# Layer 1's loop: num in the one-pass type with weights in two halves, carried rows through small transfers, and an own bank for the last columns

## The chip, the cores and the metric

The kernel runs on one core of a Trainium2 chip. The core has a matrix engine (PE, whose weight loads are listed apart as PEld), a vector engine (DVE), an activation engine (ACT), a general engine (POOL) and a queue engine that issues transfers (SP); ACT and POOL issue transfers too. All transfers run on the same 16 DMA engines. Matrix products land in PSUM, which has eight banks of 512 four-byte columns; DVE and ACT copy them to SBUF. The metric is the device time of one execution in microseconds. Three runs of the kernel before gave 651.62, 651.85 and 652.48, median 651.85.

## The reference

Two graph layers on 2708 nodes with 128 features and a dense 0/1 adjacency matrix; each ends in a layer norm. The change touches only the second one (layer 1):

```python
XW = X @ W
s_col = XW @ a[0, :f];  s_row = XW @ a[0, f:]
Z1  = leaky_relu(s_row[:, None] + s_col[None, :], 0.01)
den = exp(Z1)
num = A @ den
att = where(num != 0, den / where(num != 0, num, 1), 0)
H   = A @ (att @ XW)
out = layernorm(X + H)
```

`num` is a product of the adjacency matrix with a 2708 x 2708 matrix that depends on only two numbers per entry, s_row of one node and s_col of another.

## The kernel before

Exp(leaky_relu(a + b)) is either exp(a) exp(b) or exp(0.01 a) exp(0.01 b), and which of the two holds is decided by comparing b with -a. The kernel uses that. It sorts nodes by s_row (as "k") and by s_col (as "j") into NG = 24 groups of at most G = 126 nodes with common thresholds. Num can then be written as a running sum over the groups: for group g only the group's own 126 rows of the transposed adjacency matrix are needed, and everything outside the group is carried in two more rows, row 0 and row 1, which are the sums so far for the two branches. A group's product is therefore one 128 x 128 weight tile times a 128 x 2708 tile: 126 gathered rows plus two carried rows. Its first two output rows are the carried rows for the next group.

The stages ahead of the loop (layer 0, the sums over all nodes in `tot`, the sort, the tables) fill the first 345 us, and the last product H = A @ M with its layer norm takes the time from about 573 us on. The loop lies between them, at lines 1530 to 1589 (`for step in range(NG + LAG)`, LAG = 2).

Each step g does this. `multiply` (line 1460) forms num for six strips of 512 columns (the last has 148) with PE in the four-byte type, and DVE copies each from PSUM to the tile q. PSUM has three banks for that (`ps_num`) and five for the sums of the first five strips (`ps_m`). `carry` (1472) copies q's first two rows into rows 0 and 1 of the tile `ring` that holds the next group's gathered rows; this is one DVE instruction for three strips, twice a step. `log` (1476), on ACT, takes the logarithm of the step's q in two parts. `divide` (1480), on DVE, works on the step before: it subtracts the logarithm from the log of den. `power` (1488), on ACT, takes the exponential, in two parts and a third for the last 148 columns, which goes to a tile `tails`. `weigh` (1497) multiplies the quotient of two steps ago with that group's gathered rows of XW (`xws`) and adds it in PSUM to the sums m_acc, strip by strip. The last 148 columns have no bank of their own during the loop: `weigh_tails` multiplies all 24 of them at the end of it, in the bank m_tail. `weights` (1371) makes the weight tile of the group after next with one ACT instruction. Logarithm and exponential are in different tables of ACT, so there are two table loads a step.

POOL issues the loop's gathers: `gather` (1280), 126 rows of 10,832 bytes into one of four ring tiles, and `gather_xw` (1291), 128 rows of 512 bytes. For eleven steps it also issues a transfer that writes a two-byte copy of the first columns to HBM, and then one for `last_short`. Ring tile 0 is the room of the input x. SP issues the spread of the weights' row values over the partitions (`spread_out_weights`, 1413, for groups 4 to 7 and 8 to 23), and, as ring tiles, weights and XW rows come free, the first loads of the last product (line 1709).

The order of work on each engine is the order in the code: the helpers `mm`, `dve`, `act`, `gps` and `pinned` (lines 194 to 222) tie every instruction to the one before it on its engine, so that all of them appear under line 198 in the profile. Transfers on SP that are not pinned are placed by the scheduler by their estimated readiness. Elsewhere (`halves`, 224) a value is split into two halves of the one-pass type (F32R): the rounded value and the remainder. A product with both halves takes two one-pass products; the last product already does that with m_hi and m_lo.

## Time and profile before

| | |
|---|---|
| median of three runs | 651.85 us |
| profiled execution | 652.04 us, span 649.3 us, mean granted PE clock 0.984 |
| PE busy in the span | 608.8 us (94%) |
| DVE, ACT, POOL busy | 491.4, 471.3, 289.2 us |
| one step of the loop (from 424 us on) | 8.855 us |
| first product of num; last sums of m_acc | 345.6 us; 571.9 us |
| DMA | 171.64 MB, mean 264 GB/s |

The page sorts instructions into groups of one line, engine, operation and shape, with a count, the busy time and the mean of one; then comes the idle time of the engine before them and what ended it. A matmul of the four-byte type is two records. The records of matmuls overlap, since they are pipelined: what one costs is read from the distance between starts, not from its length. A window's row gives for each engine the busy time and the number of instructions in that stretch, then the granted clock of PE, the busy share of the DMA engines and their rate. The chain lists, in order of time, the work that set the end. A DMA row gives the time from issue to landing.

### The profile page before, as it was taken

What the parts mean: (1) busy time and instruction counts of PE and PEld (TensorE: products, weight loads), DVE (VectorE), ACT (ScalarE), POOL (GpSimd) and SP (SyncE); (2) the same over time, 40 slices, a digit from 0 to 9 for tenths busy, and PEclk for the clock granted to TensorE, in tenths of its full rate; (3) what the DMA queues carried; (4) which work ended last, traced back from release to release, by engine and by line L of the source; (5) the groups of instructions that cost most, each with busy time, mean ns of one, the idle gap of its engine ahead of it and who ended that gap; (6) DMA issues with size and microseconds to landing.
All of it is one profiled execution on the core that took longest, in us unless ns stands there. A gap on an engine that the chain in (4) does not pass through costs nothing.

```text
span 649.3 us, 8555 instructions
## 1 busy us (share of the span) xinstructions
PE 608.8 (94%) x2859; PEld 351.9 (54%) x2859; DVE 491.4 (76%) x978; ACT 471.3 (73%) x649; POOL 289.2 (45%) x270
## 2 busy tenths in 40 slices
PE   7999999999999899998878899999999999989993
PEld 4445345465655676765664344444444444658872
DVE  5765865764699756756885999899999999599575
ACT  4767786767889521410585999999999999778652
POOL 6967778777798742000123322333232230021573
PEclk9999999999999899999988999999999999999997
DMA  8968989988971999989956999756689453259981
GB/s 270 392 221 330 317 301 363 360 329 310 335 262 70 276 390 389 387 267 375 394 205 185 238 223 246 214 168 175 193 217 267 170 170 129 87 202 383 390 320 53
DMA packets 66407, 171.64 MB, mean 264 GB/s; under 512 B 10059, under 2 KB 19285, under 8 KB 63333
## 3 DMA queue, kind: packets, MB, share of 16 engines
q1 hardware_dynamic: 42500, 107.01, 46.4%
q0 software_dynamic: 22464, 62.25, 34.5%
q10 hardware_dynamic: 1392, 1.77, 0.8%
q8 instruction: 24, 0.39, 0.2%
q14 instruction: 27, 0.21, 0.1%
HBM read 171.89 MB, written 5.72 MB: 274 GB/s over the span
## 4 chain that ended last, share of the span: by engine, by line
PE 65%; ACT 13%; DVE 10%; POOL 6%; issue 4%; DMA 1%; another core or an unknown queue 0%; DVEq 0%; POOLq 0%; ACTq 0%
PE num L198 11%; PE m_acc L198 11%; PE att_acc L207 9%; PE h_acc L1690 7%; PE sim L207 7%; PE dif_acc L207 6%; ACT q L198 5%; POOL total L222 4%; ACT L198 2%; DVE q L198 2%; PE tot L198 2%; PE dif_acc L198 1%; PE sim L198 1%; POOL ss L198 1%; ACT xn L198 1%
## 5 line engine op out<-in xcount | busy, mean ns | idle before, releaser
L198 PE MATMUL m_acc<-q,xws 128*128 128x512 f32 x240 | 121.6, 592 | 0.0
L198 PE MATMUL num<-ring,wt 128*128 128x512 f32 x216 | 98.2, 546 | 3.6 <-DVE q L198 2.2
L222 POOL TENSOR_TENSOR total<-total,p_t 128x512 f32<-128x512 f32 (+1 forms) x67 | 91.8, 1370 | 21.0 <-ACT p_t L217 18.4
L207 PE MATMUL att_acc<-p_t,x_sb 128*128 128x512 f32 x184 | 91.1, 602 | 1.1 <-ACT p_t L217 1.1
L212 DVE SCALAR_TENSOR_TENSOR p_t<-sim,gentle,pieces 128x512 f32<-128x512 f32 x89 | 65.0, 746 | 34.8 <-PE sim L207 25.7
L198 DVE SCALAR_TENSOR_TENSOR q<-sr_b,nc_s,q 128x1536 f32<-128x1536 f32 (+1 forms) x48 | 77.8, 1623 | 17.3 <-ACT q L198 17.3
L217 ACT ACTIVATE p_t<-p_t,shift 128x512 f32<-128x512 f32 (+1 forms) x89 | 64.7, 745 | 33.8 <-DVE p_t L212 31.5
L198 DVE COPY q<-num 128x512 f32<-128x512 f32 (+1 forms) x142 | 83.5, 611 | 4.5 <-PE num L198 4.5
L198 PEld LDWEIGHTS m_acc<-q,xws 128*128 128x128 f32 x240 | 45.3, 190 | 55.0 <-issue 54.8
L198 ACT ACTIVATE q<-q,head,rest 128x1536 f32<-128x1536 f32 (+1 forms) x48 | 70.2, 1508 | 1.6 <-DVE ring L198 1.3
L198 ACT ACT_TABLE_LOAD x52 | 66.7, 1283 | 3.9 <-issue 3.1
L198 PEld LDWEIGHTS num<-ring,wt 128*128 128x128 f32 x216 | 39.0, 190 | 49.1 <-issue 34.2
L198 ACT ACTIVATE q<-q,c_s 128x1536 f32<-128x1536 f32 (+1 forms) x48 | 62.9, 1355 | 0.3
L198 POOL DMA_INDIRECT ring<-in_adj_t,k_no x18 | 20.8, 1154 | 89.1 <-PE num L198 85.6
L207 PEld LDWEIGHTS att_acc<-p_t,x_sb 128*128 128x128 f32 x184 | 31.7, 189 | 35.3 <-ACT p_t L217 18.8
L207 PE MATMUL sim<-xn_t 128*128 128x512 f32 x98 | 47.6, 592 | 0.0
L222 POOL TENSOR_TENSOR x<-x,p_t 128x660 f32<-128x660 f32 (+1 forms) x22 | 35.1, 1596 | 11.3 <-ACT p_t L217 10.6
L198 ACT ACTIVATE row<-row 128x1354 f32<-128x1354 f32 x30 | 39.5, 1318 | 0.3 <-DMA row<-in_adj 0.3
L207 PE MATMUL dif_acc<-strip,x_hi 128*128 128x512 f32 x88 | 37.8, 429 | 0.0
L207 PE MATMUL dif_acc<-strip,x_lo 128*128 128x512 f32 x88 | 36.2, 411 | 0.0
L1690 PE MATMUL h_acc<-rounded,m_hi 128*128 128x512 f32 x88 | 32.4, 407 | 3.7 <-DVE rounded L212 3.7
L198 PE MATMUL num<-x_sb,wt 128*128 128x512 f32 (+1 forms) x72 | 34.4, 570 | 0.7 <-ACT gb L198 0.7
(362 smaller groups left out, 1170.6 us busy)
## 6 DMA issues: line engine op xcount, KB each, us to landing
pieces<-in_adj_t SPq DMA_DIRECT2D x24, 1024.0 KB, 6.8
strip<-in_adj_t POOLq DMA_DIRECT2D x20, 1024.0 KB, 18.3
row<-in_adj SPq DMA_DIRECT2D x30, 677.0 KB, 5.5
nat<-in_adj_t SPq DMA_DIRECT2D x19, 768.0 KB, 7.7
x<-in_adj SPq DMA_DIRECT2D x14, 677.0 KB, 6.2
ring<-in_adj_t SPq DMA_DIRECT2D x9, 1024.0 KB, 5.1
pieces<-in_adj_t SPq DMA_DIRECT2D x7, 512.0 KB, 6.4
x_sb<-in_adj_t SPq DMA_DIRECT2D x4, 768.0 KB, 6.2
```

What stands on the lines that cost most here:

```text
L198: latest[engine] = op(*args, **kwargs)
L207: op(*args, **kwargs)
L212: return getattr(nc.vector, op)(*args, **kwargs)
L217: return getattr(nc.scalar, op)(*args, **kwargs)
L222: return getattr(nc.gpsimd, op)(*args, **kwargs)
L1690: nc.tensor.matmul(acc[:, : rows.shape[-1]], m[:, kb, :], rows, start=(kb, part) == (0, 0), stop=(kb, part) == (NB - 1, 1),)
```

## The change

- A group has GK = 124 gathered "k" rows instead of 126, because four carried rows take the first places instead of two: rows 0 and 1 in a rounded half and the remainder of each. The j groups keep 126. Thresholds are spaced a little closer (0.53 for 0.55), and the tables of rows are shifted accordingly.
- From group 1 on, num is two one-pass products into the same bank, with the weight tile in two halves (w_hi, w_lo); the gathered rows are 0 or 1 and are read as one-pass numbers. Group 0 stays in the four-byte type. The tiles are 2720 columns wide, so the last strip of num has 160.
- `weights` becomes four DVE instructions: scale and shift, maximum with zero, rounded half, remainder.
- `carry` is replaced by a way round for each third of the columns (1024, 1024, 672): `carry_out`, a transfer from SP that spreads q's two rows over 64 partitions of a small tile `bands`; `carry_back`, in which POOL copies the rounded half and subtracts for the remainder, and SP sends all 128 partitions back to four rows of a tile `lines`; and `carry_in_ring`, which copies `lines` to the first four rows of the ring tile, by DVE for the first third and by POOL for the other two.
- `ps_num` has two banks instead of three and `ps_m` six instead of five: the last columns have a bank of their own, and `weigh_tails` and `tails` go. `power` takes two parts.
- The order in a step is by pairs of strips: pair 0, three strips of m_acc, the division and exponential of the step before, the gather for three steps ahead (before: four), the ring copies, then pair 1, one strip of m_acc, pair 2, two strips of m_acc, DVE's ring copy, the weights and the logarithm.
- Ring tiles and the rooms of the last product are allocated anew where their type changes.

The diff, cut to what the text speaks of:

```diff
 G = 126
+GK = 124
+NC = 2720
...
-                dve("tensor_scalar", spread, spread, 0.55, None, ALU.mult)
+                dve("tensor_scalar", spread, spread, 0.53, None, ALU.mult)
...
-            out=ring[g % RING][P - G :, :],
+            out=ring[g % RING][P - GK :, :N],
...
+    carried = tab.tile([P, 2, NG], F32, name="carried")
+    for v, row in enumerate((row0, row1)):
+        low_row = tab.tile([P, 1], F32, name=f"low_row{v}")
+        gps("tensor_scalar", low_row, node[:, 0:1], v + 2.0, None, ALU.is_equal)
+        gps("tensor_tensor", low_row, low_row, row, ALU.add)
+        gps("tensor_copy", carried[:, v, :], low_row.to_broadcast([P, NG]))
+        gps("tensor_copy", carried[:, v, 0:1], row)
+    rest_k = tab.tile([P, 1], F32, name="rest_k")
+    gps("tensor_scalar", rest_k, node[:, 0:1], P - GK - 0.5, None, ALU.is_gt)
...
-    dve("tensor_scalar", kt[:, 0, :], kt[:, 0, :], rest, row0, ALU.mult, ALU.add)
-    dve("tensor_scalar", kt[:, 1, :], kt[:, 1, :], rest, row1, ALU.mult, ALU.subtract)
+    for v, op in enumerate((ALU.add, ALU.subtract)):
+        dve(
+            "scalar_tensor_tensor", kt[:, v, :], kt[:, v, :], rest_k, carried[:, v, :],
+            ALU.mult, op,
+        )
...
-    ring += [ring_p.tile([P, N], F32, name=f"ring{k}") for k in range(1, RING)]
+    ring += [
+        ring_p.tile([P, NC], F32R, tag=f"ring{k}", name=f"ring{k}") for k in range(1, RING)
+    ]
+    for t in ring[1:]:
+        gps("memset", t.bitcast(F32)[:, N:], 0.0)
...
+    wt_parts = {}
+
     def weights(g, src):
 
-        pinned(
-            "ACT", nc.scalar.activation, wt[:, g, P - G :], src, AF.Relu,
-            bias=wt[:, g, 1:2], scale=e1_s[:, g : g + 1],
-        )
+        w, e1, ne2 = wt[:, g, P - G :], e1_s[:, g : g + 1], wt[:, g, 1:2]
+        if g == 0:
+            pinned("ACT", nc.scalar.activation, w, src, AF.Relu, bias=ne2, scale=e1)
+            return
+        hi, lo = (
+            flow.tile([P, P], F32R, tag=name, name=name, bufs=3) for name in ("w_hi", "w_lo")
+        )
+        dve("tensor_scalar", w, src, e1, ne2, ALU.mult, ALU.add)
+        dve("tensor_scalar", w, w, 0.0, None, ALU.max)
+        halves(hi, lo, wt[:, g, :])
+        wt_parts[g] = hi, lo
...
-    tails = flow.tile([P, NG, N - TAIL], F32, name="tails")
-    ps_num = pool("ps_num", 3, PSUM, stack=l1)
-    ps_m = pool("ps_m", 5, PSUM, stack=l1)
+    ps_num = pool("ps_num", 2, PSUM, stack=l1)
+    ps_m = pool("ps_m", NS, PSUM, stack=l1)
...
     helped = {(0, 1), (0, 4)}
 
     def multiply(g, s, i0, i1):
+        if s == NS - 1:
+            i1 = NC
         num = ps_num.tile([P, SW], F32, tag="num", name="num")
-        mm(
-            nc.tensor.matmul, num[:, : i1 - i0], wt[:, g, :], ring[g % RING][:, i0:i1],
-            start=True, stop=True,
-        )
+        ways = [(wt[:, 0, :], ring[0])]
+        if g > 0:
+            ways = [(w, ring[g % RING]) for w in wt_parts[g]]
+        for n, (w, rows) in enumerate(ways):
+            mm(
+                nc.tensor.matmul, num[:, : i1 - i0], w, rows[:, i0:i1],
+                start=(n == 0), stop=(n == len(ways) - 1),
+            )
         to = qs[g][:, i0:i1]
         if (g, s) in helped:
             act("copy", to, num[:, : i1 - i0])
         else:
             dve("tensor_copy", to, num[:, : i1 - i0])
 
-    def carry(g, i0, i1):
-        if g + 1 < NG:
-            dve("tensor_copy", ring[(g + 1) % RING][:2, i0:i1], qs[g][:2, i0:i1])
+    bands = m_p.tile([P, SW], F32, tag="m", name="bands", bufs=2)
+    bands_r = bands.bitcast(F32R)
+    lines = {}
+
+    def carry_rows(n):
+        i0, i1 = n * 2 * SW, min((n + 1) * 2 * SW, NC)
+        c = (i1 - i0) // 32
+        return i0, i1, c, slice(n * 64, n * 64 + c), slice(n * 64 + 32, n * 64 + 32 + c)
+
+    def in_bands(t, i0, i1, c):
+        return t[:, i0:i1].rearrange("r (p c) -> r p c", c=c)
+
+    def carry_out(g, n):
+        i0, i1, c, whole, _ = carry_rows(n)
+        pinned(
+            "SP", nc.sync.dma_start, bands[:64, whole], in_bands(qs[g][:2], i0, i1, c)
+        )
+
+    def carry_back(g, n):
+        i0, i1, c, whole, split = carry_rows(n)
+        gps("tensor_copy", bands_r[:64, split], bands[:64, whole])
+        gps(
+            "tensor_tensor", bands_r[64:, split], bands[:64, whole], bands_r[:64, split],
+            ALU.subtract,
+        )
+        lines[n] = flow.tile([4, 2 * SW], F32, tag="lines", name="lines", bufs=2)
+        pinned(
+            "SP", nc.sync.dma_start, in_bands(lines[n], 0, i1 - i0, c),
+            bands_r.bitcast(F32)[:, split],
+        )
+
+    def carry_in_ring(g, n, by):
+        i0, i1, *_ = carry_rows(n)
+        by("tensor_copy", ring[(g + 1) % RING][:4, i0:i1], lines[n][:, : i1 - i0])
...
-    def quotient(g, i0, i1):
-        return tails[:, g, :] if i0 == TAIL else qs[g][:, i0:i1]
+        t = qs[g][:, i0:i1]
+        pinned("ACT", nc.scalar.activation, t, t, AF.Exp, bias=c_s[:, g : g + 1])
 
     def weigh(g, s, i0, i1):
         mm(
-            nc.tensor.matmul, accs[s][:, : i1 - i0], xws[:, g, :], quotient(g, i0, i1),
+            nc.tensor.matmul, accs[s][:, : i1 - i0], xws[:, g, :], qs[g][:, i0:i1],
             start=(g == 0), stop=(g == NG - 1),
         )
-
-    def weigh_tails(gs):
-        for g in gs:
-            weigh(g, *strips_m[-1])
...
+    def multiply_pair(g, n):
+        if g >= NG:
+            return
+        for item in strips_m[2 * n : 2 * n + 2]:
+            multiply(g, *item)
+            if (g, item[0]) == (0, 1):
+                j_no.append(numbers())
+                gather_xw(0)
+                gather(3)
+                gather_xw(1)
+        if g + 1 < NG:
+            carry_out(g, n)
+
+    def weigh_strips(g, *strips):
+        if g < 0:
+            return
+        for s in strips:
+            weigh(g, *strips_m[s])
+            if g == NG - 1:
+                to_mt(s)
+                if s > 1:
+                    m_rows(s - 2)
+
     for step in range(NG + LAG):
         g, before, first = step, step - 1, step - LAG
         if g < NG:
-            qs[g] = flow.tile([P, N], F32, tag="q", name="q", bufs=LAG + 2)
+            qs[g] = flow.tile([P, NC], F32, tag="q", name="q", bufs=LAG + 2)
+            if g > 0:
+                carry_back(g - 1, 1)
+                carry_back(g - 1, 2)
+        multiply_pair(g, 0)
+        weigh_strips(first, 0, 1, 2)
         if 0 <= before < NG:
-            for i0, i1 in (parts_m[0], (half, TAIL), (TAIL, N)):
-                power(before, i0, i1)
+            for part in parts_m:
+                divide(before, *part)
+            for part in parts_m:
+                power(before, *part)
         if g < NG:
+            if 0 < g and g - 1 + RING < NG:
+                gather(g - 1 + RING)
             if g > 0:
-                for i0, i1 in parts_m:
-                    log(g, i0, i1)
-            if 3 <= g + 2 < NG:
-                weights(g + 2, (gb[:, g + 2, :] if g < 2 else wt[:, g + 2, P - G :]))
-            if g + RING < NG:
-                gather(g + RING)
-            if g + 2 < NG:
-                gather_xw(g + 2)
+                for n in (1, 2):
+                    carry_in_ring(g - 1, n, gps)
+            if g + 1 < NG:
+                carry_back(g, 0)
+            if 0 < g < NG - 1:
+                gather_xw(g + 1)
+        if g == 0:
+            weights(1, gb[:, 1, :])
+        multiply_pair(g, 1)
+        if g == 0:
+            log(0, *parts_m[0])
+        weigh_strips(first, 3)
+        multiply_pair(g, 2)
+        if g == 0:
+            log(0, *parts_m[1])
+        weigh_strips(first, 4, 5)
+        if g == 0:
+            ring[0] = late.tile([P, NC], F32R, tag="x_sb", name="ring0")
+            gps("memset", ring[0].bitcast(F32)[:, N:], 0.0)
+        if g + 1 < NG:
+            carry_in_ring(g, 0, dve)
+        if g + 2 < NG:
+            weights(g + 2, (gb[:, g + 2, :] if g < 2 else wt[:, g + 2, P - G :]))
+        if 0 < g < NG:
+            for part in parts_m:
+                log(g, *part)
...
-        if step == NG:
-            accs.append(ps_num.tile([P, SW], F32, tag="num", name="m_tail"))
-            weigh_tails(range(first + 1))
-    weigh_tails(range(first, NG))
-    to_mt(NS - 1)
-    for s in range(NS - 3, NS):
+    for s in range(NS - 2, NS):
```

## The prediction

> **What bounds the kernel now.** I read the engine shares first, then the chain of waits, and then one period of the loop in the timeline. In the page's rows the two matmul groups of the loop are the largest. Each matmul in the full type is two records: 240 records of m_acc are 120 products.
>
> ```profile
> PE 608.8 (94%) x2859; PEld 351.9 (54%) x2859; DVE 491.4 (76%) x978; ACT 471.3 (73%) x649; POOL 289.2 (45%) x270
> ...
> L198 PE MATMUL m_acc<-q,xws 128*128 128x512 f32 x240 | 121.6, 592 | 0.0
> L198 PE MATMUL num<-ring,wt 128*128 128x512 f32 x216 | 98.2, 546 | 3.6 <-DVE q L198 2.2
> ```
>
> The chain between 440 and 460 us holds nothing but these two, each product 0.86 us after the one before, and the four-record piece that begins a period returns every 8.855 us (441.90, 450.76).
>
> ```profile
> 441.90 1.13 PE num L198 x4
> 443.03 0.86 PE m_acc L198 x2
> 443.89 0.86 PE num L198 x2
> ...
> 450.76 1.13 PE num L198 x4
> ```
>
> The windows say who else is near: in the same ten microseconds ACT is busy 9.94 and DVE 9.20, with the TensorE clock at 1.00.
>
> ```profile
> 440.00:450.00 10.00, 10.00 (x26) 4.64 (x25) 9.20 (x12) 9.94 (x10) 2.88 (x3) 1.00 0.70 194
> ```
>
> So a faster num meets ACT almost at once. ACT's period in the timeline, by starts:
>
> ```profile
> 450.61 1.28 ACT L198 ACT_TABLE_LOAD   x1
> 451.90 2.92 ACT L198 ACTIVATE q<-q,head,rest 128x1536 f32<-128x1536 f32 x2
> 454.73 0.48 ACT L198 ACTIVATE wt<-wt,kt 128x126 f32<-128x126 f32 x1
> 455.22 1.28 ACT L198 ACT_TABLE_LOAD   x1
> 456.52 2.62 ACT L198 ACTIVATE q<-q,c_s 128x1536 f32<-128x1536 f32 x2
> 459.04 0.40 ACT L198 ACTIVATE tails<-q,c_s 128x148 f32<-128x148 f32 x1
> ```
>
> **Floors of the new period.** *PE*: in the last phase two one-pass products of 512 columns start 0.47 us after the two before them, 0.235 each. Five strips in two halves are 2.35, the short strip about 0.25; m_acc keeps 5 x 0.858, plus 0.25 for the last columns (m_tail: 46 records in 5.95 us, two to a product). Sum 7.15 us, against 8.855. *ACT*: 1.29 + 2.83 + 1.30 + 2.52 stay; the weights (0.49) and the separate tail (0.42) go; the second exponential grows by 148 columns at 0.87 ns (the forms of 1536 and 1024 differ by 0.446 us), +0.13. Sum 8.07. *DVE*: five copies of 512 at 0.62 by starts and one short at 0.29 are 3.39, the two divides 1.73 + 1.35, one carried third in place of two wide rows 0.61 (the rows of 1536 and 1172 give 0.52 ns a column), and four operations on 128 columns for weights and halves, about 0.87 (0.26 by starts where two per-partition scalars are read, 0.13 to 0.26 else). Sum 7.95. *Pool*: gather and gather_xw 1.42 + 1.31 with the gaps after them, three times two small operations 0.55 (128x8 forms took 0.21 to 0.45), copies of 1024 and 672 columns 1.1 and 0.8 (1.0 to 1.3 ns a column in the casts), and 0.75 in eleven steps for the bf16 copy. About 7.0. Were these all, the period would be 8.07.
>
> **The path that sets the end is a ring.** Step g+1 multiplies a third only when two rows of step g have gone round: PE, DVE, SP out, Pool, SP back, Pool or DVE. Before, that was one DVE copy (0.95 and 0.76). For the middle third: four products of 0.235, the last one ready at 1.10 (0.40 from its start); two copies, done at 2.0; transfer out; two Pool operations 0.55; transfer back; Pool's copy of 1024 columns 1.1; five handoffs of 0.06, 0.3. That is 3.95 plus two transfers. Pool's own queue adds 0.55: between split and copy-in stand the last third's split and the gather's issue (1.42).
>
> *A small transfer from SP* is not in this loop. The nearest rows, undisturbed:
>
> ```profile
> out<-hh ACTq DMA_DIRECT2D x1, 256.0 KB, 3.0
> ...
> out<-hh POOLq DMA_DIRECT2D x1, 64.0 KB, 1.9
> ...
> out<-hh POOLq DMA_DIRECT2D x1, 10.0 KB, 1.6
> ```
>
> The 256 KB store had its first packet 1.0 us after issue. I take 2.1 us: 8 and 16 KB are nearest in size to the 10 KB, but go in 64 and 128 packets of 128 bytes. Bounds 1.6 and 3.0. The ring is 4.5 + 2 x 2.1 = **8.7 us**, just under today's 8.855.
>
> [...]
>
> *What disturbs it.* Each step's gather keeps the engines for some 4.7 us (its packets, one row of 10.8 KB each, take 0.41 us, eight to an engine: 3.3 us), and lands 7.6 us after issue. In the new order Pool issues it just before the copies-in, so the next step's first transfer out runs into it. The one small SP transfer that met gathers is the 11.8 KB store of g_d: issued at 345.23 with two gathers in flight, its follower waited
>
> ```profile
> SPq L1414 <- DMA g_d<-g_r: 6.9, 1, 6.9
> ```
>
> against 1.6 to 3.0 undisturbed: some 4 to 5 us for two gathers. For one gather and one meeting in a step: nothing (it slips through) to 3.4 (it waits for the whole gather). I take the middle, 1.7, since only one of the six transfers starts near the gather in the order of the code. Period: 8.7 + 1.7 = **10.4 us**.
>
> *Pool beside DVE.* At 574 to 577 us a Pool cast runs beside DVE casts:
>
> ```profile
> 573.35 4.03 POOL L222 CAST last<-last_short 128x1628 fp32r<-128x1628 bf16 x2 [44.27 <-PE m_tail L198]
> 573.39 2.57 DVE L212 CAST rounded<-x_sb 128x2048 fp32r<-128x2048 f32 x1
> ...
> 575.89 1.90 DVE L198 CAST m_hi<-m 128x512 fp32r<-128x512 f32 x1
> ```
>
> The same forms took 1.21 and 0.43 when Pool was still. Pool's carried work would thus cost a wait of 0 to 1.5 us in a step; within 10.4 it lies beside the gather's delay, so I add nothing and keep 1.5 for the upper end.
>
> [...]
>
> **Single costs.** *Start.* SP's queue now carries the ring, and the spread of the weights is on it: 252 KB and 1008 KB issued together at 352.6.
>
> ```profile
> wt<-g_d SPq DMA_DIRECT2D x1, 1008.0 KB, 57.4
> ...
> wt<-g_d SPq DMA_DIRECT2D x1, 252.0 KB, 6.4
> ```
>
> If the first transfers stand behind both, step 1 waits until the 1008 KB have gone. It took 57.4 us among full gathers; while the loop stands still there are few. Its 2048 packets need 4 us at the store's rate (512 in 0.95) and 16 at the rate of the 252 KB (about 125 in a microsecond). Bounds 3 and 19 over today's start; I take +10. *Wide loads on the same queue.* wt's first room (486.51), x_sb (527.91) and ring (536.80) load 1 MB each during the loop (5 us to landing), and the 814 KB of last_short (10.7 us) come from Pool. A ring transfer behind each could lose 2.5 to 3; bounds 0 and 12, I take +4. *End.* The m_tail group held the last m_acc until 567.19, though its exponentials ended at 564.63: -2.5, and 0.5 for the last tail: -3. *Before the loop* Pool gets nine small operations and three memsets, 2.2 us, beside its 2.85 us wait for tot; nothing, or 2.2 if that wait is gone. The gather of a step now goes out three steps ahead instead of four, still two periods for a landing of 7.6; nothing, unless one stalls. Num's two banks are refilled only after both copies, which the ring holds already; the wider constants and kt's changed operation are as many instructions as before. The logarithm overwrites the rows that the transfer out reads, so ACT's second one waits for the last landing, 2.1 after the last copy; ACT has 10.4 - 8.07 to spare, so nothing, and all beyond that if a landing takes 4.5.
>
> **Sum.** 22 steps x (10.4 - 8.855) = +34.0; +10 + 4 - 3 = +45. The profiled execution took 652.04 us (span 649.3 and 2.7 around it), 0.2 above the median 651.85. 652.04 + 45 - 0.2 = **697 us**.
>
> **Rivals.**
> *The ring fits (faster).* Transfers take 1.6 and slip past the gathers: ring 7.7, so ACT's 8.07 rules, in practice 8.2. 22 x (8.2 - 8.855) = -14.4, start +3, end -3: 638. For it: ACT, DVE and PE all have a floor below 8.855. Against it: the g_d wait. It decides below a period of 8.36 with my single costs (22 x 0.5 = 11), 8.86 with the least ones.
> *The ring nearly fits.* Gathers cost 0.6 a step: 9.3; 22 x 0.445 = +9.8, +11: 673.
> *Every step waits a whole gather and the DVE.* 8.7 + 3.4 + 1.5 = 13.6: +104, start and loads +20, end -3: 773. For it: the store that waited 6.9. Against: the small packets need the engines briefly.
>
> **Chances.** Forecast (period 9.7 to 12, 680 to 732) 0.45; fits 0.20; nearly fits 0.20; whole gather 0.15. The lowest tenth lies in the lower half of the first rival (640), the highest in the last one's upper two thirds (760). Within 0.2% of before, about what a measurement of this kernel can tell from no change, fall 0.02 of the first and 0.01 of the second rival: faster 0.18, same 0.03, slower 0.79.
>
> **What would show it.** num in the loop at 0.235 us by starts and gaps of PE up to a third of each period, released by Pool's or DVE's ring copy; ACT busy below 8.5 in ten; a SP transfer landing after 2 to 5 us; a first step 10 us late. I am wrong if the period is at 8.1 to 8.5 with ACT full, or if the small transfers land within 2 us whatever the gathers do.

## The result

The changed kernel takes 854.86 us (median of 4 runs, 851.75 to 863.0) against 651.74 us for the kernel before on the same chip: ratio 1.314, 95% interval 1.306 to 1.322. The prediction had 697 us and a range up to 760. The direction was right; 203 us were lost where 45 were forecast. The profiled execution took 852.16 us, its span 850.7.

The page's engine shares and largest groups, after. PE is busy 73% of the span (before 94%), and num now stands idle 179 us ahead of its first half, ScalarE's table loads 198 us, both mostly for the carried rows.

```profile
PE 618.3 (73%) x2859; PEld 374.0 (44%) x2859; DVE 507.6 (60%) x1047; ACT 458.3 (54%) x602; POOL 410.9 (48%) x467
...
L201 PE MATMUL num<-ring,w_hi 128*128 128x512 f32 x138 | 80.3, 582 | 179.1 <-DVE ring L201 108.6
L201 ACT ACT_TABLE_LOAD x52 | 66.7, 1283 | 198.1 <-DMA bands<-q 179.9
L201 PE MATMUL m_acc<-q,xws 128*128 128x512 f32 (+1 forms) x288 | 140.0, 614 | 0.0
...
L201 DVE CAST ring<-lines 4x1024 fp32r<-4x1024 f32 x23 | 15.6, 677 | 101.2 <-DMA lines<-bands 101.1
```

The page's chain of waits, by engine and by line: transfers hold 31% of it, where before it was matmuls.

```profile
PE 39%; DMA 31%; POOL 11%; DVE 7%; issue 6%; ACT 4%; SPq 0%; POOLq 0%; DVEq 0%; ACTq 0%
DMA lines<-bands 13%; PE att_acc L210 7%; DMA bands<-q 6%; PE sim L210 5%; POOL ring L201 5%; DMA wt<-in_adj_t 5%; PE num L201 5%; PE dif_acc L210 5%; PE m_acc L201 4%; DMA row_room<-in_adj_t 4%; DMA g_d<-g_r 4%; POOL total L225 3%; PE h_acc L1767 2%; DVE q L201 1%; PE tot L201 1%
```

The windows for the ten microseconds in which before had PE at 10.00, DVE at 9.20 and ACT at 9.94 (same columns: window, length, then busy time of PE, PEld, DVE, ACT, POOL, granted clock, DMA share, GB/s): nothing is full.

```profile
440.00:450.00 10.00, 6.01 (x19) 3.01 (x18) 7.66 (x12) 6.82 (x6) 5.80 (x9) 1.00 0.61 127
```

The time between steps tells more than any mean. These are the starts of each step's first copy of num in the timeline (differences in us, step 0 to 1 first):

```
before  7.7  8.1  8.6  8.6  8.9  8.9  8.9  8.9  9.6  8.9  8.9  8.9  8.9  8.9  8.9  8.9  8.9  8.9  8.9  8.9  8.9  8.8  8.9
after  27.9 29.7  9.7 11.8 12.8 25.4 10.6 12.0 12.4 29.4 10.9 11.5 14.1 27.8 14.6 16.7 17.5 26.3 10.7 11.9 11.3 15.2 14.8
```

From step 1 to step 17 every fourth step takes 25 to 30 us, and step 0 takes 28; the others take 10 to 17.5. (Step 21, in which no gather is left to issue, takes 15.2.) Up to the start of step 2 the changed kernel loses 60.1 us (423.4 against 363.3), in the 21 steps from there 141.1, in the rest 0.2: together the 201.4 by which the spans differ.

A long step in the timeline of after: three transfers are issued at 466.0, 466.65 and about 468.6, none of their readers starts before 481, and VectorE, Pool, ScalarE and PE wait 12.5 to 15 us for them.

```profile
465.99 0.56 SPq L201 DMA_DIRECT2D lines<-bands  x1
...
466.65 2.53 SPq L201 DMA_DIRECT2D bands<-q  x2
...
481.12 0.68 DVE L201 CAST ring<-lines 4x1024 fp32r<-4x1024 f32 x1 [12.54 <-DMA lines<-bands]
481.30 0.64 POOL L201 CAST bands<-bands 64x32 fp32r<-64x32 f32 x1 [13.03 <-DMA bands<-q]
481.34 1.28 ACT L201 ACT_TABLE_LOAD   x1 [15.14 <-DMA bands<-q]
```

What they wait behind is the gather. The one issued at 459.7 landed at 480.1, and the step ended 3 us later; the other four long steps of the series ended 2.5 to 3.1 us after the landing of gathers 4, 12, 16 and 20. The gather's landing in the DMA rows, before:

```profile
ring<-in_adj_t,k_no POOLq DMA_INDIRECT x18, 7.6
```

and after:

```profile
ring<-in_adj_t,k_no POOLq DMA_INDIRECT x23, 24.7
```

and the windows over a stretch in which one gather alone is under way, before (126 rows) and after (124 rows); the number ahead of GB/s is the mean busy share of the 16 DMA engines:

```profile
454.00:457.00 3.00, 3.00 (x9) 1.33 (x8) 3.00 (x3) 2.97 (x4) 0.51 (x1) 1.00 0.85 354
```

```profile
487.00:490.00 3.00, 2.78 (x11) 1.59 (x11) 2.71 (x4) 2.72 (x2) 2.51 (x4) 1.00 0.27 72
```

0.85 of 16 engines is 14, 0.27 is 4: in the packet records 14 packets of 10.8 KB are under way at once before, and 4 after. The changed group size, 124 rows for 126, left the gather 4 engines instead of 14, and each of them carries 31 rows instead of 9. A row also took longer: 354 GB/s on 14 engines is a row of 10.8 KB in 0.43 us on each, 72 GB/s on 4 is one in 0.60 us. So the rows alone take some 19 us after, two steps, where they took 3.9. (From step 2 on the packet records have 0.71 us a row in the median after, and 0.41 before, on 14 engines. Why a row is slower on 4 engines no run shows.) What is measured is the number of engines at three row counts: 14 at 126 rows, 4 at 124, and 16 at 128 (share 1.00 in the first experiment). What makes a row count take so many engines no run shows.

### The profile page after: what moved, and what is told of

Same layout as the page of the kernel before. It is cut to its first block, busy times and chain, and to the rows that moved or that the text cites. A ratio compares the mean times of both kernels' runs of the same rounds, so it can differ in the third digit from the quotient of the medians.

```text
span 850.7 us, 9207 instructions
## 1 busy us (share of the span) xinstructions
PE 618.3 (73%) x2859; PEld 374.0 (44%) x2859; DVE 507.6 (60%) x1047; ACT 458.3 (54%) x602; POOL 410.9 (48%) x467
## 4 chain that ended last, share of the span: by engine, by line
PE 39%; DMA 31%; POOL 11%; DVE 7%; issue 6%; ACT 4%; SPq 0%; POOLq 0%; DVEq 0%; ACTq 0%
DMA lines<-bands 13%; PE att_acc L210 7%; DMA bands<-q 6%; PE sim L210 5%; POOL ring L201 5%; DMA wt<-in_adj_t 5%; PE num L201 5%; PE dif_acc L210 5%; PE m_acc L201 4%; DMA row_room<-in_adj_t 4%; DMA g_d<-g_r 4%; POOL total L225 3%; PE h_acc L1767 2%; DVE q L201 1%; PE tot L201 1%
## 5 line engine op out<-in xcount | busy, mean ns | idle before, releaser
L201 PE MATMUL num<-ring,w_hi 128*128 128x512 f32 x138 | 80.3, 582 | 179.1 <-DVE ring L201 108.6
L201 PE MATMUL m_acc<-q,xws 128*128 128x512 f32 (+1 forms) x288 | 140.0, 614 | 0.0
L201 PEld LDWEIGHTS num<-ring,w_hi 128*128 128x128 f32 x138 | 33.2, 241 | 220.7 <-DVE ring L201 113.1
L201 POOL CAST bands<-bands 64x32 fp32r<-64x32 f32 (+1 forms) x69 | 19.5, 282 | 156.9 <-DMA bands<-q 156.2
L201 PEld LDWEIGHTS m_acc<-q,xws 128*128 128x128 f32 x288 | 60.7, 219 | 45.2 <-issue 39.3
L201 POOL CAST ring<-lines 4x1024 fp32r<-4x1024 f32 (+1 forms) x46 | 65.8, 1451 | 25.3 <-DMA lines<-bands 24.5
L201 DVE CAST ring<-lines 4x1024 fp32r<-4x1024 f32 x23 | 15.6, 677 | 101.2 <-DMA lines<-bands 101.1
L201 PE MATMUL num<-ring,w_lo 128*128 128x512 f32 x138 | 62.4, 462 | 0.0
L201 POOL DMA_INDIRECT ring<-in_adj_t,k_no x23 | 38.6, 1677 | 15.8 <-issue 12.3
L201 POOL DMA_INDIRECT xws<-xw_d,j_no x24 | 25.3, 1055 | 33.4 <-DVE c_s L201 22.8
```

What stands on the lines that cost most here:

```text
L201: latest[engine] = op(*args, **kwargs)
```

## The experiments

Each shows its edit against the kernel named. All but the second are built on the changed kernel. "128 rows" stands for the kernel of the first experiment.

**Gathers of 128 rows.** Four rows of zeros more, at the places that the carried rows fill later.

```
-            out=ring[g % RING][P - GK :, :N],
+            out=ring[g % RING][:, :N],
...
-            in_offset=bass.IndirectOffsetOnAxis(ap=k_no[:GK, g : g + 1], axis=0),
+            in_offset=bass.IndirectOffsetOnAxis(ap=k_no[:, g : g + 1], axis=0),
```

> Every gather of adjacency rows fetches 128 rows instead of 124; the four rows more are a row of zeros, at the places that the carried rows fill later, and the output is the same. Theory A: what the prediction missed is that 124 rows go on 4 DMA engines where 126 went on 14 (at 487 us the trace of the changed kernel shows 4 packets of 10.8 KB under way at once, before shows 14 at 447 us), so that a gather holds its engines for 13 us and more and the small transfers on the same engines wait one long packet for each of their own. With 128 rows on 16 engines the landing of a gather falls from 24.7 us to 6 to 9, the store of g_d from 30 us to 5 to 9, the steps of 25 to 30 us (six of them, about 16 us too much in each) vanish: 852 - 22 - 6 x 16 = about 735 us, and 690 to 710 if the other steps also fall from 12 to 10.4 as predicted. Rival B: the small transfers wait behind the queue of SyncE and Pool whatever the gathers do: the long steps stay and the time is above 820 us.

746.5 us, ratio to before 1.144 (1.138 to 1.151): 108 us of the 203 were the number of rows. The landing is back (DMA rows; then a window over one gather, on all 16 engines):

```profile
ring<-in_adj_t,k_no POOLq DMA_INDIRECT x23, 7.5
```

```profile
462.00:464.00 2.00, 2.00 (x7) 1.25 (x6) 1.33 (x2) 0.91 (x1) 1.46 (x4) 0.65 1.00 379
```

No step is above 15.4 us after the first. But the steps from 2 on still take 12.8 us in the mean, not 10.4, and theory A's 690 to 710 did not come; its 735, for the long steps alone, was 12 short.

**The kernel before with 124 rows.**

```
+        n = G if g < RING else G - 2
...
-            out=ring[g % RING][P - G :, :],
+            out=ring[g % RING][P - G : P - G + n, :],
...
-            in_offset=bass.IndirectOffsetOnAxis(ap=k_no[:G, g : g + 1], axis=0),
+            in_offset=bass.IndirectOffsetOnAxis(ap=k_no[:n, g : g + 1], axis=0),
```

> The kernel before, with gathers of 124 rows in place of 126 from the fifth gather on; the last two rows of each group are left as they were, so the sums lack them. Nothing else is changed. Theory A: a gather now lasts 31 packets of 0.41 us on 4 engines, 13 us, longer than a step of 8.855 us, but it has four steps and nothing small waits behind it, and successive gathers lie on different engines: the landing goes from 7.6 us to 13 to 16, the time changes by 0 to +10 us. If every gather used the same four engines, the step would be 13 us and the time about 652 + 19 x 4.5 = 737 us. Rival B (the number of rows is of no account): 652 us, landing 7.6.

697.45 us, ratio 1.072 (1.066 to 1.078): 47 us from two rows fewer (38 to 56 by run), with no small transfer in the loop. The landing is 26.4 us, past the 13 to 16 that I expected from 0.41 us a row: in this run's packet records a row takes 0.75 us in the median, so 31 of them take 23. Num waits for rows in five steps of 12 to 17.5 us; most others stay at 8.8 to 9.0.

```profile
ring<-in_adj_t,k_no POOLq DMA_INDIRECT x18, 26.4
```

**Why every fourth step.** Gathers 0, 4, 8, ... on 16 engines, the others on 4 as in the changed kernel.

```
+        n, no = (P, k_no_wide) if g % 4 == 0 else (GK, k_no)
-            out=ring[g % RING][P - GK :, :N],
+            out=ring[g % RING][P - n :, :N],
```

> The changed kernel (854.9 us), in which every fourth gather (0, 4, 8, 12, 16, 20, those into the first ring slot) fetches 128 rows, on 16 engines, and the others 124, on 4, as they are. In the changed kernel the steps of 25 to 30 us are those from the issue of gathers 4, 8, 12, 16 and 20 on. Theory R: gathers on 4 engines take the next 4 in turn, and the transfers of the carried rows always the same few, so one gather in four meets them. If the gathers on 16 engines don't count in that turn, the meetings move: every fourth of the gathers 1, 2, 3, 5, 6, 7, 9, ... meets, so 6, 11, 17 and 22 or a like series, and long steps come 5 to 6 apart, near steps 3, 8, 14 and 19; the time falls only by the shorter start and one long step less, to 780 to 835 us. Theory S: it is the first ring slot (its address), or its gathers, that meets: all long steps go, and the time is 745 to 770 us.

835.0 us, and the long steps after the start are 3, 8, 14 and 19 (24.9, 31.2, 31.1 and 26.4 us), those in which gathers 6, 11, 17 and 22 are issued: theory R's series, number for number, and not theory S's. (Step 0 takes 37.0 us, which theory R did not forecast.) This fits gathers on 4 engines that take the next four in turn, and transfers of the carried rows that always take the same few; but the records do not name a packet's engine, so it stays the author's explanation of the series. That two gathers do not share four engines the packet records of after show: between 463 and 470 us, where the gathers issued at 447.3 and 459.7 overlap, mostly eight or nine rows are under way at once, and about four after 471.

**Fewer, larger packets.** In the changed kernel, 8 bands for 32 (a transfer back in two, hi and lo).

```
-        c = (i1 - i0) // 32
+        c = (i1 - i0) // 8
...
-            "SP", nc.sync.dma_start, bands[:64, whole], in_bands(qs[g][:2], i0, i1, c)
+            "SP", nc.sync.dma_start, bands[:16, whole], in_bands(qs[g][:2], i0, i1, c)
```

> The changed kernel as it is (gathers of 124 rows, 854.9 us), with each carried third cut into 8 bands in place of 32: a transfer out is 16 packets of 512 bytes instead of 64 of 128, and a transfer back two of 16 packets instead of one of 128. Theory G: on an engine that a gather holds, packets of the two queues take turns, so each small packet waits for one row of 0.43 us; 32 small packets on an engine are 14 us (at 474 to 478 us of the changed kernel 8 to 11 of them went in a microsecond beside as many rows, on about four engines), 8 are 3.5. Then the long steps of 25 to 30 us fall to 15 to 19, five of them, and the first steps lose some too: 770 to 800 us. Rival H: a small transfer waits until the gather's own rows are done, however many packets it has: 845 to 860 us.

861.81 us (844.44 to 863.46), which its four runs don't tell from the changed kernel's 851.75 to 863.0, and far from theory G's 770 to 800; the long steps from step 5 on stayed at 25 to 28 us. With 128 rows and 4 bands:

> The kernel with gathers of 128 rows (746.5 us), with each carried third cut into 4 bands in place of 32: 8 packets of 1 KB out, two transfers of 8 packets back. By theory G (turns of one row and one packet) a transfer that meets a gather waits 4 rows, 1.7 us, in place of all 8, 3.4 us: a step is 1 to 1.7 us shorter, less 0.2 to 0.5 for Pool's two longer operations: 715 to 735 us. By rival H, 745 to 760.

753.46 us, 7 us more than with 32 bands. Theory G's numbers failed. The runs don't settle whether the two queues' packets take turns, and no record shows how many packets of a burst meet a gather on one engine with 8 bands. The packet records of the long step shown above fit theories G and H in part each: none of the burst's 256 packets goes before 471, 61 of them go from 471 to 478 beside 60 rows, and the other 195 after that, when five rows are left. What the two runs show is that larger bands don't help.

**What the rest is worth without the ring.** The carried rows' way round is left out; constants stand in the ring, and gathers are of 112 rows, which landed in 7.8 us in the median (of 128 rows: 7.5).

```
-                carry_back(g - 1, 1)
-                carry_back(g - 1, 2)
...
-            carry_in_ring(g, 0, dve)
```

> The changed kernel with gathers on 16 engines (112 rows, so 12 rows of each group are left out) and without the whole way round of the carried rows: no transfer out, no split, no transfer back, no copy into the ring; constant ones stand in their place, so the sums lack what is carried. This is the floor of everything else. If the floors of the prediction hold, ScalarE rules with 8.07 to 8.3 us a step: 22 x (8.2 - 8.855) = -14, the end -3, the start about 0 to +5: 636 to 642 us. If Pool or VectorE has a floor of its own that the prediction missed, steps of 9 us or more and above 655 us.

652.23 us, ratio 1.001 (0.999 to 1.004). The steps are 8.26 us in the mean, ScalarE is full (window of ten microseconds), as the prediction's floor says:

```profile
440.00:450.00 10.00, 8.70 (x29) 4.93 (x30) 9.18 (x15) 9.94 (x8) 2.83 (x3) 1.00 0.85 190
```

The loop's 21 steps win 12.9 us and the end 2.5; up to step 2 it loses 14.2, part of it this experiment's own four fills of the ring (2.33 us of VectorE each, 9.3 in all). So all but the ring could be worth up to 9 us; the next run, which carries the rows, has nothing left of it.

**The carried rows copied straight, rounded.**

```
+            by("tensor_copy", ring[(g + 1) % RING][:2, i0:i1], qs[g][:2, i0:i1])
...
-            dve("tensor_copy", to, num[:, : i1 - i0])
+            dve("tensor_scalar", to, num[:, : i1 - i0], TINY, None, ALU.max)
```

> The changed kernel with gathers of 128 rows, in which the carried rows take no way round: VectorE copies the first third and Pool the other two straight into the ring, rounded to the one-pass type in one part; the copies of num have a lower bound of 1e-18. The low halves of the carried rows are left out, so the sums are less exact. All else (one-pass num, weights by VectorE in two halves, own bank) is there. The prediction's floors are ScalarE 8.07, VectorE 7.95, Pool 7.0 a step, and 8.3 was measured without any carry: 22 x (8.3 - 8.855) = -12, the end -2 or -3, the start 0 to +3: 636 to 642 us, 1.5 to 2% faster than before. If Pool's copies beside VectorE cost what the casts at 574 us showed (0 to 1.5 us a step), up to 9.3 a step and 660.

654.44 us, ratio 1.006 (1.004 to 1.008): no gain even with no transfer in the ring. Most steps are 8.8 to 8.9 (9.0 in the mean), and VectorE is the engine with the least rest, 9.53 of ten microseconds busy (window, then VectorE's timeline). The second of the four operations on the weights takes 0.65 us beside Pool's copy, where it takes 0.23 to 0.42 in the runs in which no such copy is beside it, and the first third's carry adds 0.67.

```profile
440.00:450.00 10.00, 8.61 (x31) 5.11 (x30) 9.53 (x17) 9.43 (x7) 6.78 (x7) 1.00 0.62 173
```

```profile
449.11 0.65 DVE L201 TENSOR_SCALAR wt<-wt 128x126 f32<-128x126 f32 x1
...
450.27 1.28 DVE L201 TENSOR_SCALAR q<-num 128x512 f32<-128x512 f32 x2
451.47 3.16 DVE L201 SCALAR_TENSOR_TENSOR q<-sr_b,nc_s,q 128x1536 f32<-128x1536 f32 x2
454.54 0.67 DVE L201 CAST ring<-q 2x1024 fp32r<-2x1024 f32 x1
```

**The remaining 12.8 us a step.** A step of the kernel with 128 rows, Pool and SyncE: the middle third's copy-in (460.44) stands behind the last third's way out (454.1 to 456.9), its split and a gather's issue of 2.40 us. (A row with "DMA_INDIRECT" on POOL is the time in which Pool issues a gather.)

```profile
456.90 0.20 POOL L201 CAST bands<-bands 64x21 fp32r<-64x21 f32 x1 [1.74 <-DMA bands<-q]
457.18 0.23 POOL L201 TENSOR_TENSOR bands<-bands 64x21 fp32r<-64x21 f32 x1
...
457.99 2.40 POOL L201 DMA_INDIRECT ring<-in_adj_t,k_no  x1 [0.58 <-issue]
...
460.44 1.94 POOL L201 CAST ring<-lines 4x1024 fp32r<-4x1024 f32 x2
```

Two new orders of Pool, on 128 rows. First (split 1, gather, copy-in 1, split 2, gather of xw, copy-in 2, split 0):

> The kernel with gathers of 128 rows (746.5 us, 12.8 us a step), and Pool's order within a step changed: split of the middle third, gather, copy-in of the middle third, split of the last third, gather of xw, copy-in of the last third, split of the first third; before, both splits and the gather stood ahead of the first copy-in. Theory C: the ring that closes is longer than the one in the prediction, because Pool works in order: the middle third's copy-in stood behind the last third's way out and split and behind the gather's issue (at 457 to 462 us of that run: transfer out 2.8, split 0.5, gather 2.4 with 0.6 before it, two copies). Then a step falls by 1.5 to 2.5 us, to 10.3 to 11.3, and the time by 33 to 55 us, to 690 to 715. Rival D: the transfers' own delay by gathers and the bf16 copy rules, whichever third is last: the step stays at 12 to 13, 735 to 750 us.

800.28 us, 54 more. The new order hit SyncE's queue: the transfer out of the middle third was ready when the copies of num ended at 496.25, but stood behind the first third's transfer back, whose split I had moved to the end. It was issued at 499.83. So this run doesn't test theory C.

```profile
494.98 1.27 DVE L201 COPY q<-num 128x512 f32<-128x512 f32 x2
...
495.45 4.28 SPq L201 DMA_DIRECT2D lines<-bands  x2
...
499.83 1.25 SPq L201 DMA_DIRECT2D bands<-q  x2
```

Second, the gather's issue alone moved behind the copies-in:

> The kernel with gathers of 128 rows, with only the gather's issue moved on Pool: behind the two copies-in and the first third's split instead of ahead of them. Theory C says the gather's issue (1.4 to 2.4 us) leaves the chain: 22 x 1.5 to 2.5 less, 690 to 715 us, unless its rows then meet the transfers out of the middle and last third (up to 3.4 us, the prediction's bound for one meeting): then 730 to 780. Rival D: within 15 us of 746.

766.48 us, 20 more: the rows now stand before the last third's way out, and its split waits 4.68 us.

```profile
435.78 0.20 POOL L201 CAST bands<-bands 64x21 fp32r<-64x21 f32 x1 [4.68 <-DMA bands<-q]
```

**Short rows**, on 128 rows:

```
+        n = N if g < RING else D
...
-            out=ring[g % RING][P - GK :, :N],
+            out=ring[g % RING][:, :n],
...
-            in_=adj_t[:, :],
+            in_=(adj_t if g < RING else xw_d)[:, :],
```

> The kernel with gathers of 128 rows (746.5 us, 12.8 us a step), in which every gather from the fifth on fetches 128 short rows of 0.5 KB of another table in place of the 10.8 KB rows of the adjacency; Pool issues the same instruction. The sums are therefore not the kernel's; copies of num have a lower bound of 1e-18. Theory F: in that kernel what is left of the excess over a step of 8.7 is the gather's long packets, which hold all 16 engines for 3.4 to 4 us, in whose way one transfer out always stands, wherever Pool issues the gather (moved behind the copies-in, it cost 13.1 a step as well). Then a step falls by 2 to 3.5 us, to 9.3 to 10.8, and the time to 670 to 702. Rival: Pool's instructions and SyncE's in-order queue set the step, the long rows do not matter: 735 to 750 us.

737.12 us: 9 less, not 45 to 75. With the gather's issue moved as well:

> The kernel with short gather rows (737 us, 12.1 us a step) and with the gather's issue moved behind the copies-in and the first third's split, as in the run with the gather last. Each of these two edits alone brought at most 9 us (737) or cost 20 (766). Theory K: a step pays for the gather once in either place, either by its issue on Pool (0.6 to 0.7 of idle and 1.9 to 2.4, between the last third's split and the middle third's copy-in, on the ring) or, moved away from there, by its long rows, which then stand before the last third's transfer out (4.7 us of waiting at 431 us of that run). With both gone a step falls by 2.3 to 3 us, to 9.1 to 9.8, near the 8.7 of the prediction's undisturbed ring: 670 to 688 us. Rival L: the ring is long for a reason that has nothing to do with the gather (the last third's way out and split ahead of the middle third's copy-in, and the transfers themselves): 720 to 740 us.

729.5 us (a step is 11.9 in the mean from step 2 on, not the 11.1 of a later expectation). Theory K fell; the time is in rival L's range. What is left in that run's chain is Pool: two gathers' issues of 1.02 us each (at 577.23 and 578.56), now ahead of the middle third's split, and its copy-in, which takes 2.66 us beside VectorE's divide.

```profile
577.23 1.02 POOL ring L201
...
578.56 1.02 POOL xws L201
...
580.56 2.44 DMA lines<-bands
...
583.05 2.66 POOL ring L201
```

**Pool beside the divide**, on 128 rows: the copy-in of the middle third by ScalarE (`nc.scalar.copy` between its two table loads), and a divide with one tensor as input:

```
...
-            "scalar_tensor_tensor", t, sr_b[:, i0:i1], nc_s[:, g : g + 1], t,
-            ALU.max, ALU.subtract,
...
+        dve("tensor_scalar", t, t, -1.0, nc_s[:, g : g + 1], ALU.mult, ALU.add)
```

> The kernel with gathers of 128 rows (746.5 us, 12.8 us a step), in which ScalarE and not Pool copies the middle third into the ring, between its two table loads. Theory M: what makes the ring 12.4 and not 8.7 is Pool beside VectorE's divides: the same Pool copy of 4x1024 took 1.0 us with VectorE still and 2.1 to 2.7 beside a divide, a gather's issue 1.0 and 2.4, and both stand before the middle third's num. With ScalarE's copy (about 0.9 us, done near 460 instead of 461.7 in the step that begins at 449) the step falls by 1.3 to 2 us: 703 to 718 us. Rival N: the transfers and SyncE's queue rule; the copy's place is no matter, and ScalarE, held by it, gives the gain back: 735 to 755.

> The kernel with gathers of 128 rows (746.5 us), in which VectorE's divide is an operation with one tensor as input in place of two (the tensor of row maxima is left out, so the weights are not the kernel's). Pool's order is as it was. [...] If an operation of one input holds Pool up as well: at most the divide's own gain shows, and Pool's longest copies stay above 2 us: 725 to 747.

745.45 and 737.75 us: 1 and 9 less. Both miss the times that theory M gave, 703 to 718 and 692 to 715 us; the second run shows a part of the gain on Pool that it forecast (in the mean the copy falls from 1.56 to 1.19 us, the gather's issue from 1.65 to 1.27). In ten steps of the first run and eight of the second the chain goes by the first third, whose transfer out meets the gather's rows and takes 5.4 to 6.6 us. The chain of the run with one input:

```profile
587.16 5.93 DMA bands<-q
...
593.70 2.32 DMA lines<-bands
...
596.11 0.69 DVE ring L201
```

**All three out**: short rows, gather behind the copies-in, divide with one input.

> All three disturbances of the ring are out of the kernel with gathers of 128 rows: short rows from the fifth gather on, the gather's issue behind the copies-in and the first third's split, and a divide with one input (both left-out parts make the sums another's). Two of the three together gave 729.5 us and 11.1 us a step, the one-input divide alone 737.75 and 11 to 12.5. Theory P: there are three rings, one to a third, and each disturbance lengthens another of them by about 3 us (the gather's issue and the slowed copies that of the middle third, the long rows that of the third whose transfer out they meet), so that taking one out uncovers the next; without all three a step is the sum of its undisturbed pieces, num 1.2, copies to 2.4, 0.6 for the transfer back in front on SyncE, out 2.2, split 0.5, back 2.4, copy-in 1.0 and handoffs: 9.3 to 9.8 us, and the time 685 to 700 us. Rival Q: the transfers' own times or something else rule: the step stays at 10.8 to 11.4 and the time at 722 to 732 us.

705.83 us, ratio 1.084 (1.079 to 1.090), 41 less than with 128 rows and 6 above theory P's range. Where neither a bf16 copy (Pool's transfer that writes the two-byte copy) nor a wide load (1 MB or so for the last product) runs, a step is 9.4 to 9.5 us (steps 16, 17, 19 and 20), which is theory P's sum for a step. With the bf16 copies (steps 3 to 13) it is 10.7 in the mean, with a wide load 11 to 13; no run leaves the copies or the loads out. One of the short steps in the timeline, by the middle third from num at 564.46 to num at 573.97, 9.51 us. The first transfer is the first third's way back, which stands ahead on SyncE's queue; the next two are the middle and the last third's way out:

```profile
564.46 0.50 PE L201 MATMUL num<-ring,w_hi 128*128 128x512 f32 x1 [0.34 <-POOL ring L201]
...
565.23 1.29 DVE L201 TENSOR_SCALAR q<-num 128x512 f32<-128x512 f32 x2 [0.20 <-PE num L201]
...
566.14 0.56 SPq L201 DMA_DIRECT2D lines<-bands  x1
...
566.80 1.74 SPq L201 DMA_DIRECT2D bands<-q  x2
...
569.03 0.58 POOL L201 CAST bands<-bands 64x32 fp32r<-64x32 f32 x1
...
569.70 0.25 POOL L201 TENSOR_TENSOR bands<-bands 64x32 fp32r<-64x32 f32 x1
...
569.97 1.32 SPq L201 DMA_DIRECT2D lines<-bands  x2
...
572.77 2.38 POOL L201 CAST ring<-lines 4x1024 fp32r<-4x1024 f32 x2 [2.25 <-DMA lines<-bands]
...
573.97 0.50 PE L201 MATMUL num<-ring,w_hi 128*128 128x512 f32 x1 [0.67 <-POOL ring L201]
```

And Pool's copy of 4x1024 (groups by form: busy, mean ns), with 128 rows:

```profile
L201 POOL CAST ring<-lines 4x1024 fp32r<-4x1024 f32 x23 | 35.8, 1557 | 23.6 <-DMA lines<-bands 23.0
```

and here:

```profile
L201 POOL CAST ring<-lines 4x1024 fp32r<-4x1024 f32 x23 | 27.3, 1186 | 56.8 <-DMA lines<-bands 56.7
```

The traces put a price on Pool beside the divide without any edit: in the kernel with 128 rows the 6 copies of 4x1024 that no divide overlaps take 1.03 us each and the other 17 take 1.75 in the mean; in the run with short rows and the gather moved it is 1.03 (7 copies) and 2.04 (16).

So each third has its ring, the disturbances lengthen different ones by about as much, and the longest shows: alone they were worth 9 (rows), -20 (issue moved) and 9 us (second input), together 41. Which third closes the ring in which run is read from the chains; no run takes one third's way round out.

**The start**, on 128 rows: the spread of the weights issued at the end of step 3, and then also VectorE for ScalarE's two copies of step 0 (`helped = set()`).

> The kernel with gathers of 128 rows, with the 1008 KB spread of the weights issued on SyncE's queue at the end of step 3 instead of before step 0's second transfer. The first two steps take 17.8 and 14.4 us in that run, against 7.7 and 8.1 in the kernel before: 16.4 us. If the prediction's term for the start (+10, bounds 3 to 19) is what this load costs, they fall by 8 to 14 us together, and step 3 or 4 pays 3 to 5 of it: 735 to 742 us. If the start is slow for another reason (ScalarE's copy of one strip stands behind a logarithm that waits for the transfer out), they fall by less than 4 us: 742 to 750.

> The kernel with the late spread of the weights (746.7 us; first two steps 14.0 and 14.9 us against 7.7 and 8.1 before), in which VectorE and not ScalarE copies two of step 0's strips. Theory: the start is slow because ScalarE's copy of the fifth strip stands behind the first logarithm, which overwrites rows that the transfer out still reads and so waits 6 us for its landing; without it the first step falls by 3 to 6 us: 740 to 744 us. If something else holds the start: 745 to 748.

746.7 and 745.46 us, no difference from 746.5 that the spread of these kernels' runs (7 to 15 us) lets one tell. In the profiles the first two steps fell from 32.2 to 28.9 and 25.2 us, against 15.8 before; neither cause alone is the start's.

## Why the prediction was wrong, and where it was right

- **The gather (wrong, 108 us).** The failed step is "Each step's gather keeps the engines for some 4.7 us ... eight to an engine ... and lands 7.6 us after issue": durations of before, carried over to a transfer whose row count the diff changes from 126 to 124. The runs showed 31 rows to an engine, a landing of 24.7 us, and 108 us less with 128 rows. ("Eight to an engine" was not right for before either: 126 rows on 14 engines are nine.) The term for the gather that goes out three steps ahead instead of four, "nothing, unless one stalls", rested on the same 7.6.
- **The undisturbed ring (8.7; measured 9.5).** In the step shown and in its like (16 and 19) the middle third is copied 2.06 us after its first product (2.0 in the sum), waits 0.3 for a transfer back that stands ahead on SyncE's queue (not in the sum), is split 2.2 after the issue of its way out (2.1), in 0.9 (0.55), and is copied in 2.8 after the issue of its way back (2.1), in 1.2 (1.1). So the way out was right and the way back 0.7 short, though the last packets of both came 1.6 to 1.8 us after issue. Against that, the sum's 0.55 for Pool's own queue is not in these steps.
- **What disturbs it (+1.7; measured 12.8 - 9.5 = 3.3).** Long rows, the gather's issue and the divide with two inputs make 2.1 of it (12.8 to 10.7); 1.2 is the difference between that run's mean step and its short ones, in which no bf16 copy or wide load runs. Pool's own queue, 0.55 in the sum, should have been a ring of its own: the middle third's copy-in waits for the last third's way out. To add the delay of one meeting to one path was wrong too; there were three paths.
- **Pool beside DVE (0; 1.1 a step).** From 729.5 to 705.8 us over 22 steps, with the other two disturbances gone. The casts at 574 us, from which the prediction had 0 to 1.5 us a step, spoke against the zero, and the runs bear them out in kind: between these two runs Pool's copy of 4x1024 falls from 1.73 us in the mean with two-input divides to 1.19 with one-input ones. Part of the 1.1 need not be Pool's delay: the two divides of a step are themselves 1.4 us shorter with one input (1.02 + 1.01 against 1.82 + 1.66).
- **Start (+10, bounds 3 to 19).** 60 us in the changed kernel, 16.8 with 128 rows. Of the 60, 18 are lost before the first copy of num, whose gather landed 28.1 us after issue; 20 in step 0, where the store of g_d took 30 us and the first transfer out stood on SyncE's queue behind the load that waits for it; and 22 in step 1, which meets gather 4. So a transfer did stand behind a load, but not for the 1008 KB of the prediction: with 128 rows, moving that load to step 3 did not change the time. What makes up the 16.8 stays open. A DMA row and the chain of after:

```profile
x_sb<-in_adj_t,k_no POOLq DMA_INDIRECT x1, 28.1
```

```profile
346.81 30.43 DMA g_d<-g_r
...
377.29 0.40 SPq L1442
...
377.85 4.61 DMA bands<-q
```

- **Wide loads (+4, bounds 0 to 12).** About 12, the upper bound: in the run with all three out, the steps with or just after a load are 11.6, 12.2, 11.5, 11.0 and 12.9 us against 9.4: 2.2 + 2.8 + 2.1 + 1.6 + 3.5. In the changed kernel they can't be told apart from the gathers.
- **End (-3).** -2.5 and -2.2 in the two runs without the ring, right; +0.2 in the changed kernel, where the last steps still hold the ring.
- **Floors.** ScalarE's 8.07 is 8.26 to 8.3, close to the 8.2 that the first rival had in practice. VectorE's 7.95 is 8.8 to 8.9 when the rows are carried by its and Pool's copies. So that rival's 638 us was out of reach: with no transfer in the ring the kernel is at 654.
- **The logarithm's wait (0).** ScalarE's 198 us of idle, 180 of them for a transfer out, are the ring's stall seen from ScalarE: no run took that wait alone away, so whether it adds anything stays open.
- **The rivals.** The nearest one, every step waiting for a whole gather, had 773 us at 0.15. Its mechanism came true in every fourth step, with a gather that landed 20 to 25 us after issue in place of a wait of 3.4.

No version here beats the kernel before. Undisturbed, the ring is 9.5 us against the 8.855 it had to beat; with the rows copied straight, VectorE holds the step at 8.8 to 8.9. Slower was thus right for the reason that the prediction gave, the ring, but more than half of the loss came from the gather's engines, which it did not have.

## What to carry to other kernels

When a diff changes the number of rows of a transfer, measure its number of engines again before anything else, by the DMA share over one transfer alone: two rows fewer cost 47 us in a kernel otherwise unchanged, and 108 us where small transfers waited behind them. A ring of small transfers has one path per piece and per in-order queue; draw all of them, since taking out one disturbance shows only the next, and price each with the other queues' work in front of it. Before building a detour, measure the loop without it: here the kernel that copies the rows straight was no faster than before.

## What the runs showed that was not expected

- Long steps came at every fourth step, and at 3, 8, 14 and 19 when one gather in four had 128 rows: as if gathers on few engines took the next engines in turn and those on 16 did not count.
- The same Pool copy of 4x1024 took 1.0 to 2.65 us, the same gather's issue 1.0 to 2.6, the copy 1.03 whenever no divide ran beside it (in the runs with two-input divides).
- PE's granted clock was lower in the run in which PE was more idle, a mean of 0.984 before (94% busy) and 0.869 after (73%); a num product that starts 0.235 us after the last at clock 1.00 went at 0.43 just after a long stall (482.44, 482.87, 483.30), at a granted clock of 0.50.
